# A state-space layer and a gated recurrence in one kernel: two groups' recurrences side by side in the convolution

## The chip, the cores and the metric

The kernel runs on one core of one Trainium2 chip. The metric is the device time of one execution in microseconds; the time before is the median of three runs, 2799.89 us (2799.45 to 2800.06). The core has five engines that each work through a queue of their own in order: TensorE (PE, matmuls, with PEld for its weight loads), VectorE (DVE), ScalarE (ACT), GpSimd (POOL) and SyncE (SP), which here issues nearly all DMA transfers.

## The reference

Input x is [8, 2048, 512]: 8 batch rows, 2048 positions, 512 channels. Two blocks follow each other, each with a layer norm before and after and the input added:

```
x = x + layernorm(S4(layernorm(x)))
x = x + layernorm(FFN(layernorm(x)))
```

S4 is a diagonal-plus-low-rank state-space layer with 64 states. Its convolution kernel K of length 2048 for each channel is made from the parameters, and it computes

```
h1 = irfft(rfft(r, 2L) * rfft(K, 2L))[:, :L]
return gelu(h1 + D[0] * r, approximate=False)
```

FFN reads the first axis as time (T = 8 steps here, with 2048 rows):

```
def step(c, xt):
    ft = sigmoid(xt @ wf.T + c @ uf.T + bf)
    it = sigmoid(xt @ wi.T + c @ ui.T + bi)
    gt = tanh(xt @ wc.T + c @ uc.T + bc)
    return ft * c + it * gt
c_final = scan(step, c0, x)
return tanh(x @ wo.T + c_final @ uo.T + bo)
```

c0 is one vector in_c for all rows, so its products with uf, ui and uc are three vectors of 512 that join the biases at the first step.

## The kernel before

**First stage (to about 150 us).** From the S4 parameters it computes the transition matrix A of a chunk of 128 positions and its powers, split into two float16 halves ("hi" and "lo"); all later S4 products are three float16 matmuls, hi x hi, lo x hi, hi x lo (`mm3`, L448). Beside it, `stats` (L584) loads the whole input in 32 tiles of 1 MB, through five buffers in turn, and computes means and variances: for chunk j, DVE takes nd rows of eight (`ND`, five from the sixth chunk on) and ACT the others. It also normalises groups 0 and 1 and runs their recurrences. This stage's order is chosen by a scheduler, not by hand.

**Convolution stage (to about 630 us).** The 512 channels are 16 groups of 32. The 2048 positions are 16 chunks of 128. A group needs:

- its normalised input `u`: two loads `xg` of 1 MB, then for eight pairs of chunks a subtraction on POOL (L640), a multiply on DVE (L642), a copy to float16 on ACT (L644) and the low half on POOL (L646). This is `norm_x`; it is done two groups ahead.
- the recurrence over chunks, `chain_in`, `chain_hi`, `chain_lo` (L648 to L667): for 15 chunks j, PSUM gets three products of u (L450 to L452), two with the high half of the state before (L660), and one with its low half (L666). Then `split` (L100) writes the new state x: ACT copies it to float16 (L101), DVE subtracts to get the low half (L102). Step j + 1 needs both.
- taps: `tap_steps`, twelve doublings that make 128 taps `m` for each half of the group, each with a `split`; a copy from `mb` on POOL (L682) comes first, and a 1 MB load t of the kernel's Toeplitz form (L679).
- the convolution itself: 32 calls of `conv_mm` (L698), one for a channel, six matmuls each, and eight Gelu evictions on ACT (L716), after which SP stores 2 MB of y.

In iteration g of the loop at L807, PE does the convolution of group g, in 16 slots s_ of two calls, and between them the recurrence of group g + 1, one step a slot: the high products between the two calls, the low one after the second, and the input products of the next step at the slot's end. `norm_x` for group g + 2, the taps for g + 1 and `work` stand at hand-written slots. For PE, ACT, DVE and POOL the order within an iteration is the program's order; work of neighbouring iterations may be placed across their border by the scheduler. SP's order is the scheduler's. Two pools hold the states x of two groups.

`work` is what the second block needs later. `weight_pieces` (L387) turns seven weight matrices, in 14 pieces, into Strassen-like sums with scaled float16 halves and stores them to `wf_d`: a load `wl` (512 KB), four sums on DVE in a buffer `ws` (L404, L405 in slot 2; L408, L409 in slot 5), `plain` in slot 8 (three blocks without sums, L392 on ACT and L393 on DVE, one store) and `summed` in slot 12 (four blocks, one store). The load for the next piece is issued in slot 9. `first_piece` (L442), in slot 14 of groups 1 to 12, loads 128 rows of uf, ui or uc (256 KB) and multiplies them with in_c, summing along the row (L446).

**Second block (from about 630 us).** The gate matmuls of `part_a` and `part_b` run with PE nearly without a pause; the change touches only names of buffers there.

## Time and profile before

| what | value |
|---|---|
| median of three runs | 2799.89 us |
| the profiled execution | 2797.84 us, span 2796.0 us |
| first stage, to the first convolution matmuls | about 146 to 150 us |
| convolution groups 1 to 14 | about 165 to 600 us |
| DVE, ACT, POOL busy in 300 to 400 us | 81.1, 65.9, 75.1 us |
| PE busy in 300 to 400 us | 83.3 us |
| DMA share in 300 to 400 us | 0.83, 257 GB/s |
| DMA share and rate in 0 to 140 us | 274 GB/s on average |
| L102 on DVE, one low half of x (128x256) | 0.42 us |
| L101 on ACT, one high half of x | 0.38 us |

A busy share is the part of a stretch in which the engine runs instructions. A wait is the idle time of an engine just before an instruction, put down to what released it last. In a row of the timeline the columns are start and duration in us, engine, line, operation, output and input tiles, their shapes, a count of merged instructions and, in brackets, the idle time before with its releaser. "x" is the state of the recurrence, "pxt" its PSUM tile, "m" and "pmt" taps, "pyt" the convolution's PSUM tile, "u" the normalised input, "wl", "ws", "wr", "wq" a weight piece, its sums and its converted blocks, "un" rows for the c0 products.

### The profile page before, as it was taken

Reading aid. Unit: us, or ns where it says so; the run is one execution under the profiler, and the core shown is the slowest. Engines: PE = TensorE matmul, PEld = TensorE weight load, DVE = VectorE, ACT = ScalarE, POOL = GpSimd, SP = SyncE. Lnnn points to the kernel's source line nnn. Section 1 sums busy time; section 2 is a strip of 40 time slices with the busy share of each in tenths; the row PEclk is TensorE's granted clock in tenths of the full one; section 3 lists DMA queues with packets and bytes.
Section 4 is the critical chain, followed back from the end, with each engine's and each line's share of the span. In section 5 each row is a group of like instructions: output and inputs, shape, how many; then the busy total and the mean of one; then the engine's idle time right before and its main releaser. Section 6 shows DMA issues by size and latency. Waiting matters only on the chain.

```text
span 2796.0 us, 59846 instructions
## 1 busy us (share of the span) xinstructions
PE 2538.4 (91%) x23892; PEld 2225.9 (80%) x23892; DVE 2076.8 (74%) x4208; ACT 1474.4 (53%) x3075; POOL 1224.0 (44%) x1520
## 2 busy tenths in 40 slices
PE   4578888896999999999999999999999999999990
PEld 3367777785888888888888887888888788888880
DVE  8878888867667766577887777778777577776748
ACT  8966666654444444445555544455555445544436
POOL 5767777743112211114554531355544124543317
PEclk9799999998999999999999999999999999999995
DMA  6977887887335433235665532355554335543247
GB/s 237 311 232 243 256 257 245 260 282 208 106 75 132 113 90 85 95 91 142 162 178 150 144 103 91 108 165 170 155 165 134 95 94 154 165 124 102 91 168 250
DMA packets 507535, 449.24 MB, mean 161 GB/s; under 512 B 275574, under 2 KB 386680, under 8 KB 502264
## 3 DMA queue, kind: packets, MB, share of 16 engines
q1 hardware_dynamic: 506824, 444.90, 52.9%
q8 instruction: 186, 3.05, 0.4%
q14 instruction: 93, 0.76, 0.1%
q10 hardware_dynamic: 432, 0.52, 0.1%
HBM read 293.58 MB, written 151.78 MB: 159 GB/s over the span
## 4 chain that ended last, share of the span: by engine, by line
PE 63%; DVE 6%; ACT 3%; issue 1%; POOL 1%; DMA 1%; SPq 0%; POOLq 0%; DVEq 0%; ACTq 0%
PE u L955 61%; PE pt L485 2%; DVE u L997 1%; DVE zz L1187 1%; ACT gate L1021 1%; ACT xf L101 0%; PE u L450 0%; DVE sth L462 0%; DVE u2p L994 0%; DVE xf L102 0%; PE u L452 0%; PE u L451 0%; DVE cd L1042 0%; ACT zr L1153 0%; ACT cf L1064 0%
## 5 line engine op out<-in xcount | busy, mean ns | idle before, releaser
L955 PEld LDWEIGHTS <-w 128*128 128x128 f16 x15120 | 1480.8, 98 | 203.2 <-issue 18.9
L955 PE MATMUL u<-xf,w 128*128 128x256 f16 x8064 | 944.1, 273 | 22.9 <-ACT gate L1021 9.6
L955 PE MATMUL u<-cf,w 128*128 128x256 f16 x7056 | 825.6, 273 | 1.2 <-DVE cf L1066 1.2
L1021 ACT ACTIVATE gate<-u,bias 128x512 f32<-128x512 f32 (+1 forms) x384 | 201.0, 574 | 282.4 <-PE u L955 282.1
L993 ACT ACTIVATE u2p<-u 128x256 f32<-128x256 f32 x256 | 96.6, 379 | 425.2 <-PE u L955 425.0
L955 PE MATMUL u<-w,xf 128*128 128x256 f16 x2688 | 310.8, 273 | 3.7 <-DVE u L997 3.7
L1154 POOL TENSOR_TENSOR x1r<-x1r,zr 128x512 f32<-128x512 f32 x96 | 133.5, 1391 | 407.4 <-ACT zr L1153 298.8
L994 DVE TENSOR_TENSOR u2p<-u2p,u 128x256 f32<-128x256 f32 x256 | 106.7, 417 | 275.2 <-ACT u2p L993 273.7
L909 POOL TENSOR_TENSOR xr<-y,xr 128x512 f32<-128x512 f32 x120 | 160.6, 1358 | 304.0 <-ACT y L908 304.0
L955 PEld LDWEIGHTS <-xf 128*128 128x128 f16 x2688 | 263.2, 98 | 36.1 <-DVE u L997 5.2
L997 DVE TENSOR_TENSOR u<-u,u2p 128x512 f32<-128x512 f32 x256 | 179.0, 699 | 8.8
L646 POOL TENSOR_TENSOR u<-xg,u 128x512 f16<-128x512 f32 x104 | 129.1, 1241 | 107.6 <-ACT u L644 106.6
L471 POOL TENSOR_TENSOR rsy<-rsy,nhalf 128x2 f32<-128x2 f32 (+1 forms) x68 | 50.2, 739 | 283.2 <-DVE rsy L465 282.0
L640 POOL TENSOR_TENSOR xg<-xg,mu 128x512 f32<-128x512 f32 x112 | 162.3, 1455 | 6.7 <-DMA xg<-in_xr 6.7
L102 DVE TENSOR_TENSOR x<-pxt,x 128x256 f16<-128x256 f32 x240 | 100.0, 418 | 63.6 <-ACT x L101 62.2
L1026 DVE SCALAR_TENSOR_TENSOR gate<-gate,gate 128x1024 f32<-128x1024 f32 x64 | 90.0, 1406 | 69.5 <-ACT gate L1021 68.3
L1136 POOL TENSOR_TENSOR zr<-zr,ur 128x512 f32<-128x512 f32 x96 | 131.2, 1367 | 21.1 <-DMA zr<-z_d 12.7
L462 DVE BATCH_NORM_STATS2 sty<-y 128x6 f32<-128x512 f32 x120 | 76.9, 681 | 77.1 <-DMA y<-y_d 77.1
L666 PE MATMUL pxt<-x,at 128*128 128x256 f16 x224 | 61.8, 276 | 79.4 <-DVE x L102 78.8
L101 ACT ACTIVATE x<-pxt 128x256 f16<-128x256 f32 x240 | 91.5, 382 | 74.4 <-PE pxt L666 68.7
L451 PE MATMUL pyt<-u,t 128*128 128x128 f16 (+2 forms) x544 | 124.0, 228 | 0.0
L452 PE MATMUL pyt<-u,t 128*128 128x128 f16 (+2 forms) x544 | 123.5, 227 | 0.0
(375 smaller groups left out, 5204.8 us busy)
## 6 DMA issues: line engine op xcount, KB each, us to landing
xs<-in_rr SPq DMA_DIRECT2D x32, 1024.0 KB, 6.0
t<-kpad SPq DMA_DIRECT2D x32, 1024.0 KB, 5.6
y_d<-y SPq DMA_DIRECT2D x30, 1024.0 KB, 7.6
xr<-in_r SPq DMA_DIRECT2D x60, 512.0 KB, 5.5
xa<-x_d SPq DMA_DIRECT2D x120, 256.0 KB, 4.0
y<-y_d SPq DMA_DIRECT2D x59, 512.0 KB, 5.9
x_d<-xr SPq DMA_DIRECT2D x59, 512.0 KB, 3.2
xg<-in_xr SPq DMA_DIRECT2D x28, 1024.0 KB, 8.2
```

The source lines that it names most:

```text
L102: V.tensor_tensor(lo, src, hi, ALU.subtract)
L451: T.matmul(out, lhsT=w(1), rhs=x(0), start=False, stop=False)
L452: T.matmul(out, lhsT=w(0), rhs=x(1), start=False, stop=stop)
L640: Q.tensor_tensor(xg, xg, bc(mu1), ALU.subtract)
L646: (V if g == 2 else Q).tensor_tensor(u[:, js, 1], xg, u[:, js, 0], ALU.subtract)
L909: Q.tensor_tensor(xv, yv, xv, ALU.add)
L955: T.matmul(u[:, d], lhsT=w(f, b, i == 1, k), rhs=x(f, b, i == 2, k), start=opens and bank not in seen, stop=stop and j == len(n) - 1, skip ...
L994: V.tensor_tensor(u2, u2, u[:, UY], ALU.add)
L997: V.tensor_tensor(u[:, 2:4], u[:, 2:4], u2[:, None].to_broadcast([P, 2, BP]), ALU.add)
L1021: act = lambda o, s_, b: S.activation(o, s_, AF.Tanh, scale=gsc[kind], bias=b)
L1136: Q.tensor_tensor(s_["z"], s_["z"], us_[c], ALU.add)
L1154: Q.tensor_tensor(s_["x"], s_["x"], s_["z"], ALU.add)
```

## The change

- The recurrence of group c is no longer done in one iteration. Its steps 0 to 6 are done in iteration c - 2 at positions 11, 14, 18, 21, 25, 28, 31 (a position is one `conv_mm`, two a slot), its steps 7 to 14 in iteration c - 1 at positions 3, 6, 10, 13, 16, 20, 23, 27. So two recurrences stand side by side. At each position the input, high and low products follow each other. Group 2 runs in iteration 1 alone, at every odd position; group 3 has four steps in iteration 1 and eleven in iteration 2. A third buffer for x (pool `cx`) is added.
- To make room, the four sums of a weight piece are made in place in `wl`, after the plain blocks, which stand first now; the halves of a row are swapped at loading, by two loads. The conversions are four instead of three on each of ACT and DVE, in slots 2, 3, 13 and 14, with four stores from two buffers (`wr`, `wq`) in turn; the sums stand in slots 5, 7, 9 and 11. The next piece's load is issued after slot 14.
- The c0 products leave the convolution. Their rows are loaded in the first stage, three at a time (768 KB), into the tile `ya`, which is not used yet then, at chunks 8, 9, 11 and 12, and multiplied at chunks 10 to 13, three each.
- Buffers of the second block that shared tags with `un`, `ws` and `c0r` move to a pool `FJ2`, opened when `cx` and `cr` are closed.

```diff
+    puc = const.tile([P, 3, KT], F32, name="puc")
...
         def load():
             wl = wjob[w, i] = FJ.tile([P, 2, H], F32, name="wl")
-            dma(out=wl, in_=a["wt"][w].rearrange("(a k) p m -> p k a m", a=2)[:, i])
+            wsrc = a["wt"][w].rearrange("(a k) p m -> p k a m", a=2)[:, i]
+            dma(out=wl[:, :, BP:], in_=wsrc[:, :, 0:BP])
+            dma(out=wl[:, :, 0:BP], in_=wsrc[:, :, BP:])
 
         def sums(part):
             wl = wjob[w, i]
+            a21, a11, a22, a12 = wl[:, 0, 0:BP], wl[:, 0, BP:], wl[:, 1, 0:BP], wl[:, 1, BP:]
+            o, x, y, op = ((a11, a11, a21, ALU.subtract), (a21, a21, a22, ALU.add), (a22, a22, a11, ALU.subtract), (a12, a12, a22, ALU.subtract))[part]
+            V.tensor_tensor(o, x, y, op)
+
+        def plain(part):
+            wl = wjob[w, i]
             if part == 0:
...
+                wr = FJ.tile([P, 2, 2, BP], F16, name="wr")
+                halves((wr[:, :, 0], wr[:, :, 1]), wl[:, :, BP:], sc)
+                dma(out=wf_d[WORDER.index(w), :, i, 0:2], in_=wr)
             else:
...
+                wr = FJ.tile([P, 2, BP], F16, name="wr", tag="wq")
+                halves((wr[:, 0], wr[:, 1]), wl[:, 1, 0:BP], -sc)
+                dma(out=wf_d[WORDER.index(w), :, i, 2], in_=wr)
+
+        def summed(part):
+            wl = wjob[w, i] if part == 0 else wjob.pop((w, i))
+            wq = FJ.tile([P, 2, 2, BP], F16, name="wq", tag="wq" if part else "wr")
+            halves((wq[:, :, 0], wq[:, :, 1]), wl[:, :, part * BP : (part + 1) * BP], sc)
+            dma(out=wf_d[WORDER.index(w), :, i, 3 + 2 * part : 5 + 2 * part], in_=wq)
...
+    def c0_load(n):
+
+        dma(out=yw[:, 1 + n % 2 * 3 : 4 + n % 2 * 3], in_=a["un"].rearrange("g m p h -> p (g m) h")[:, 3 * n : 3 * n + 3])
+
+    def c0_product(n):
+
+        v = yw[:, 1 + n % 6]
+        tc.keep_in_program_order(V.scalar_tensor_tensor(v, v, 1.0, yw[:, 0], ALU.mult, ALU.mult, accum_out=puc[:, n // KT, n % KT : n % KT + 1]))
...
-                xs_[g] = (ce, cb)[g % 2].tile([P, NJ - 1, 2, GB], F16, name="x", bufs=1)
+                xs_[g] = (cb, cx, ce)[g % 3].tile([P, NJ - 1, 2, GB], F16, name="x", bufs=1)
...
         for j in range(NJ):
+            if j == 8:
+                dma(out=yw[:, 0], in_=a["c0r"])
+            if j in (8, 9, 11, 12):
+                c0_load((8, 9, 11, 12).index(j))
             stats(j)
+            if 10 <= j < 14:
+                for n in range(3):
+                    c0_product(3 * (j - 10) + n)
...
-        JS = (2, 5, 8, 12)
+        JS = (2, 3, 5, 7, 9, 11, 13, 14)
...
+        HEAD, REST = (11, 14, 18, 21, 25, 28, 31), (3, 6, 10, 13, 16, 20, 23, 27)
+        steps(1, 2, 0, range(1, 2 * NJ - 1, 2))
+        steps(1, 3, 0, (18, 22, 26, 30))
+        steps(2, 3, 4, (2, 4, 7, 9, 12, 14, 17, 19, 22, 24, 27))
+        for c in range(4, NG):
+            steps(c - 2, c, 0, HEAD)
+            steps(c - 1, c, len(HEAD), REST)
+
+        def chain_at(g, p):
+            for c, j in chain.get((g, p), ()):
+                chain_in(c, j)
+                chain_step(c, j)
...
                     conv_mm(g, 2 * s_)
-                    if ahead and s_ < NJ - 1:
-                        chain_hi(g + 1, s_)
+                    chain_at(g, 2 * s_)
                     conv_mm(g, 2 * s_ + 1)
-                    if ahead and s_ < NJ - 1:
-                        chain_lo(g + 1, s_)
+                    chain_at(g, 2 * s_ + 1)
                     if ahead and 1 <= s_ <= 12:
                         tap_step(*taps[s_ - 1])
-                    if ahead and s_ < NJ - 2:
-                        chain_in(g + 1, s_ + 1)
                     for f in work.get((g, s_), ()):
                         f()
```

`yw` is the tile `ya` seen as rows of 512 channels; `at`, `work` and `conv_mm` are as before.

More of the change, by code (lines that the diff above doesn't have):

```diff
@@ L108, in s4_gated_block @@
     cb = kctx.enter_context(tc.tile_pool(name="cb", bufs=2))
-    ectx, mctx, rctx, pctx = ExitStack(), ExitStack(), ExitStack(), ExitStack()
+    ectx, mctx, rctx, xctx, pctx = ExitStack(), ExitStack(), ExitStack(), ExitStack(), ExitStack()
     ce = ectx.enter_context(tc.tile_pool(name="ce", bufs=1))
@@ L396, in load @@
             wl = wjob[w, i] = FJ.tile([P, 2, H], F32, name="wl")
-            dma(out=wl, in_=a["wt"][w].rearrange("(a k) p m -> p k a m", a=2)[:, i])
+            wsrc = a["wt"][w].rearrange("(a k) p m -> p k a m", a=2)[:, i]
+            dma(out=wl[:, :, BP:], in_=wsrc[:, :, 0:BP])
+            dma(out=wl[:, :, 0:BP], in_=wsrc[:, :, BP:])
         def sums(part):
             wl = wjob[w, i]
-            a11, a21, a12 = wl[:, 0, 0:BP], wl[:, 0, BP:], wl[:, 1, 0:BP]
+            a21, a11, a22, a12 = wl[:, 0, 0:BP], wl[:, 0, BP:], wl[:, 1, 0:BP], wl[:, 1, BP:]
@@ L402, in sums @@
+            o, x, y, op = ((a11, a11, a21, ALU.subtract), (a21, a21, a22, ALU.add), (a22, a22, a11, ALU.subtract), (a12, a12, a22, ALU.subtract))[part]
+            V.tensor_tensor(o, x, y, op)
+        def plain(part):
+            wl = wjob[w, i]
             if part == 0:
-                ws = wjob["s", w, i] = FJ.tile([P, 4, BP], F32, name="ws")
-                V.tensor_tensor(ws[:, 0], a21, wl[:, 1, BP:], ALU.add)
-                V.tensor_tensor(ws[:, 2], a11, a21, ALU.subtract)
-            else:
-                ws = wjob["s", w, i]
-                V.tensor_tensor(ws[:, 1], ws[:, 0], a11, ALU.subtract)
-                V.tensor_tensor(ws[:, 3], a12, ws[:, 1], ALU.subtract)
@@ L411, in plain @@
-        def plain():
-            wl = wjob.pop((w, i))
-            wr = FJ.tile([P, 3, 2, BP], F16, name="wr")
-            halves((wr[:, 0:2, 0], wr[:, 0:2, 1]), wl[:, :, 0:BP], sc)
-            halves((wr[:, 2, 0], wr[:, 2, 1]), wl[:, 1, BP:], -sc)
-            dma(out=wf_d[WORDER.index(w), :, i, 0:3], in_=wr)
-        def summed():
-            ws = wjob.pop(("s", w, i))
-            wq = FJ.tile([P, 4, 2, BP], F16, name="wq")
-            halves((wq[:, :, 0], wq[:, :, 1]), ws, sc)
-            dma(out=wf_d[WORDER.index(w), :, i, 3:7], in_=wq)
@@ L424, in weight_pieces @@
-        return load, lambda: sums(0), lambda: sums(1), plain, summed
+                wr = FJ.tile([P, 2, 2, BP], F16, name="wr")
+                halves((wr[:, :, 0], wr[:, :, 1]), wl[:, :, BP:], sc)
+                dma(out=wf_d[WORDER.index(w), :, i, 0:2], in_=wr)
+            else:
+                wr = FJ.tile([P, 2, BP], F16, name="wr", tag="wq")
[6 more added lines that the diff above has]
+            dma(out=wf_d[WORDER.index(w), :, i, 3 + 2 * part : 5 + 2 * part], in_=wq)
@@ L426, in out_pieces @@
+        order = ((plain, 0), (plain, 1), (sums, 0), (sums, 1), (sums, 2), (sums, 3), (summed, 0), (summed, 1))
+        return [load] + [lambda f=f, part=part: f(part) for f, part in order]
     def out_pieces(i):
@@ L440, in out_pieces @@
         return load, split_
-    def first_piece(gt, m):
-        un = FJ.tile([P, H], F32, name="un")
-        dma(out=un, in_=a["un"][gt, m])
-        V.scalar_tensor_tensor(un, un, 1.0, c0r, ALU.mult, ALU.mult, accum_out=puc[:, gt, m : m + 1])
+    def c0_load(n):
[3 more added lines that the diff above has]
+        tc.keep_in_program_order(V.scalar_tensor_tensor(v, v, 1.0, yw[:, 0], ALU.mult, ALU.mult, accum_out=puc[:, n // KT, n % KT : n % KT + 1]))
     def mm3(out, w, x, start=True, stop=True):
@@ L485, in forms @@
                 T.transpose(pt[h][:, k], xa[h][:, k * P : (k + 1) * P], ident)
-        b1 = FJ.tile([P, 2, 2, P], F32, name="b1", tag="un")
-        ts = FJ.tile([P, 4, 2, P], F32, name="ts", tag="ws")
+        b1 = FJ2.tile([P, 2, 2, P], F32, name="b1")
+        ts = FJ2.tile([P, 4, 2, P], F32, name="ts", tag="ws")
         for h in range(2):
@@ L548, in sum_ @@
             if t and cj % 2 == 0:
-                x1 = FJ.tile([P, H], F32, name="x1e", tag="ws" if cj else "wr")
+                x1 = (FJ2 if cj else FJ).tile([P, H], F32, name="x1e", tag="ws" if cj else "wr")
             early["x1", cj] = x1
@@ L557, in xnorm @@
             if cj == 1:
-                normed["o"] = FJ.tile([P, 2, H], F32, name="xa1", tag="wq")
+                normed["o"] = FJ2.tile([P, 2, H], F32, name="xa1", tag="wq")
             x = normed[cj] = normed["o"][:, cj // 2] if cj % 2 else FE.tile([P, H], F32, name="xa", bufs=2)
@@ L578, in s4_gated_block @@
     ya = cb.tile([P, QC, H // HS, 2, HS], F32, name="ya", bufs=1)
+    yw = ya.rearrange("p c (k a) t h -> p (c k) (a t h)", k=2)
     with ExitStack() as cctx:
@@ L766, in s4_gated_block @@
             split(mb[:, 0, k, :], mb[:, 1, k, :], pmt)
+        cx = xctx.enter_context(tc.tile_pool(name="cx", bufs=1, reuse_waits="tile"))
         for g in range(2):
@@ L780, in s4_gated_block @@
         jobs = [weight_pieces(w, i) for w in WORDER for i in range(2)]
-        firsts = [(gt, m) for gt in range(3) for m in range(KT)]
-        JS = (2, 5, 8, 12)
+        JS = (2, 3, 5, 7, 9, 11, 13, 14)
         work = {}
@@ L788, in s4_gated_block, with steps @@
         for n, job in enumerate(jobs):
-            if n < NG - 3:
-                at(n + 1, 0 if n == 0 else -1, job[0])
-                for s_, f in zip(JS, job[1:]):
-                    at(n + 1, s_, f)
-                if n + 1 < NG - 3:
-                    at(n + 1, 9, jobs[n + 1][0])
-            else:
-                s0 = 5 * (n - NG + 3)
-                for k, f in enumerate(job):
-                    at(NG - 2, s0 + k, f)
-        for n, (gt, m) in enumerate(firsts):
-            at(n + 1, 14, lambda gt=gt, m=m: first_piece(gt, m))
+            if n == 0:
+                at(1, 0, job[0])
+            for k, (s_, f) in enumerate(zip(JS, job[1:])):
+                at(n + 1, s_ if n < NG - 3 else k, f)
+            if n + 1 < len(jobs):
+                at(n + 1, 14, jobs[n + 1][0])
+        chain = {}
+        def steps(g, c, j0, ps_):
+            for j, p in enumerate(ps_, j0):
+                chain.setdefault((g, p), []).append((c, j))
+        HEAD, REST = (11, 14, 18, 21, 25, 28, 31), (3, 6, 10, 13, 16, 20, 23, 27)
[9 more added lines that the diff above has]
+                chain_step(c, j)
         for g in range(NG - 1):
@@ L811, in s4_gated_block @@
                 FJ = ctx.enter_context(tc.tile_pool(name="fj", bufs=1, side="right", reuse_waits="tile"))
-                c0r = FJ.tile([P, H], F32, name="c0r")
-                dma(out=c0r, in_=a["c0r"])
-                puc = FJ.tile([P, 3, KT], F32, name="puc")
             if g == NG - 2:
+                xctx.close()
                 rctx.close()
+                FJ2 = ctx.enter_context(tc.tile_pool(name="fj2", bufs=1, side="right", reuse_waits="tile"))
                 FW = ctx.enter_context(tc.tile_pool(name="fw", bufs=1, side="right", reuse_waits="tile"))
@@ L830, in s4_gated_block @@
                     taps = tap_steps(g + 1)
-                    chain_in(g + 1, 0)
                 if nn:
@@ L987, in part_a @@
         else:
-            g = gates[key] = FJ.tile([P, 4, BP], F32, name="gate2", tag="wq") if kind == 2 else FT.tile([P, 4, BP], F32, name=f"gate{kind}")
+            g = gates[key] = FJ2.tile([P, 4, BP], F32, name="gate2", tag="wq") if kind == 2 else FT.tile([P, 4, BP], F32, name=f"gate{kind}")
             c22 = g[:, 2]
@@ L1180, in load_x @@
             else:
-                s_["x"] = (FJ, FJ, FE, FT, FJ, FT)[i - 3].tile([P, 2, H], F32, name="xx", tag=("wl", "ws", "y", "gate1", "wq", "gate0")[i - 3])
+                s_["x"] = (FJ, FJ2, FE, FT, FJ2, FT)[i - 3].tile([P, 2, H], F32, name="xx", tag=("wl", "ws", "y", "gate1", "wq", "gate0")[i - 3])
             dma(out=s_["x"], in_=x1_d[c, :, 2 * tp : 2 * tp + 2])
@@ L1216, in s4_gated_block @@
         V.scalar_tensor_tensor(bias0[:, gt], puc[:, gt], 1.0 if gt == 2 else 0.5, bias[:, gt], ALU.mult, ALU.add)
-    u2p, u2s = FJ.tile([P, 2, BP], F32, name="u2p", tag="c0r"), []
+    u2p, u2s = FJ.tile([P, 2, BP], F32, name="u2p", tag="wq"), []
     todo = {}
```

## The prediction

> **What bounds the kernel now.** I read the page first (which engine is full, and where), then busy time by stage, then the waits of the matrix engine, then the timeline around the longest of them.

> ```profile
> span 2796.0 us, 59846 instructions
> PE 2538.4 (91%) x23892; PEld 2225.9 (80%) x23892; DVE 2076.8 (74%) x4208; ACT 1474.4 (53%) x3075; POOL 1224.0 (44%) x1520
> 232.60:264.45 31.85, 26.62 (x319) 22.95 (x317) 25.77 (x45) 21.02 (x46) 23.59 (x21) 1.00 0.81 253
> 296.35:328.20 31.85, 26.62 (x320) 22.95 (x318) 25.78 (x45) 21.02 (x46) 23.57 (x21) 1.00 0.81 253
> PE pxt L666 <- DVE x L102: 68.0, 65, 4.9
> PE pxt L660 <- ACT x L101: 2.9, 10, 1.5
> ```

> TensorE carries the whole run; the change touches the first 620 us only. The two rows with a colon are two convolution groups (length, then busy us of PE, PE's weight loads, DVE, ACT, POOL, then clock, DMA share and GB/s): a group takes 31.85 us, TensorE works 26.62 of it at clock 1.00, DVE 25.8, POOL 23.6. The idle 5.2 us is almost all one wait: between 160 and 600 us the last matmul of a recurrence step (L666) waited 65 times, 68.0 us in all, for the low half of the step before it (L102 on DVE). The next rows show why that half is late at a group's end (PE's last convolution matmul of this group ends near 328.2).

> ```profile
> 327.03 0.63 ACT L644 ACTIVATE u<-xg 128x512 f16<-128x512 f32 x1 [1.50 <-DVE xg L642]
> 327.74 1.16 POOL L646 TENSOR_TENSOR u<-xg,u 128x512 f16<-128x512 f32 x1 [2.43 <-ACT u L644]
> 328.85 1.24 POOL L682 COPY m<-mb 128x128 f16<-128x128 f16 x1
> 329.67 2.84 POOL L640 TENSOR_TENSOR xg<-xg,mu 128x512 f32<-128x512 f32 x2
> 324.70 1.70 DVE L393 SCALAR_TENSOR_TENSOR wq<-ws,wq 128x1024 f16<-128x1024 f32 x1 [0.26 <-ACT wq L392]
> 326.32 0.68 DVE L642 TENSOR_TENSOR xg<-xg,rs 128x512 f32<-128x512 f32 x1
> 331.31 1.75 DVE L642 TENSOR_TENSOR xg<-xg,rs 128x512 f32<-128x512 f32 x1 [0.83 <-POOL xg L640]
> 332.98 0.41 DVE L102 TENSOR_TENSOR x<-pxt,x 128x256 f16<-128x256 f32 x1
> 333.45 0.27 PE L666 MATMUL pxt<-x,at 128*128 128x256 f16 x1 [1.02 <-DVE x L102]
> ```

> DVE runs its queue in order. A normalisation multiply (L642) waits for POOL's subtraction, which waits for a copy that waits for the group's end; the recurrence's low half stands behind it and PE stands still. The same multiply takes 0.68 us while POOL waits and 1.75 while POOL works.

> **The sum's base.** The profiled execution took 2797.84 us, 1.84 more than its span; the median of the three runs is 2799.89. I work out differences from the profile and take them from the median.

> **Part 1, two recurrences side by side (groups 2 to 13, twelve of them).** Nothing is removed: 15 steps a group stay. What changes is the distance. A convolution position is six matmuls, 0.34 us (302.14 to 302.48 in PE's timeline); the three input products of a step take 0.33, its two high products 0.22, the low one 0.11. Before, steps were two positions apart; now three or four, with the other chain's steps between in mid-group. A step's latency is ACT 0.38, DVE 0.42 and about 0.3 of hand-over, 1.1 us; from position 10 to 28 the distance is 2.5 us or more, so 1.3 us of DVE lateness is absorbed. The two longest stalls there now, 1.58 and 0.97 us, come from 2.57 us (L404 and L405 together) and 1.92 us (both L393 of the plain parts) on DVE; the change also spreads these over slots. I cost the stalls of mid-group at nothing.

> At the group's end the cover is gone. In the order of the changed program, PE does the convolutions of positions 0 to 3 of the next group before the low product of the step at 31, and then the step at 3 at once; no matmul lies between the two. On DVE the low half of step 31 stands behind the first multiply (L642) of the next group. With 0 at PE's last matmul of position 31: PE reaches step 3 at 0.33 + 4 x 0.34 + 0.22 + 0.33 + 0.11 = 2.4. That multiply ended at 331.31 + 1.75 = 333.06 in the rows above, 4.86 after 328.2; the low half after it ends at 5.27. POOL's order at this place is the same (L646, copy, two L640). So PE stands 5.27 - 2.4 - 0.22 (high products) = 2.7 us. Bounds: 1.1 (the latency alone, if the multiply is in time) and 3.3 (POOL half a microsecond later, because its L646 now waits for an ACT copy behind 0.62 us of weight conversion and a 0.69 us Gelu). I take 2.7, because the rows are of this place.

> The second place is position 10. ACT's queue after step 3 (5.7 to 6.1) holds a Gelu 0.69, a copy (L644) 0.63, two small ones, and then the first weight conversion of the group, 0.62: done near 8.4. DVE takes the low part of that conversion (L393, 128x512: 1.43 us) and another multiply (0.8) before it comes to step 6: ready at 10.9. PE gets to its low product of step 10 at 5.4 + 1.8 + 2.3 = 9.5. That is 1.4; bounds 0 and 1.4, taken 1.0, since some of ACT's queue can run while PE stands at step 3. Together 3.7 us against 5.2: 1.5 us a group, **-18 us**; bounds 1.1 and 5.2, that is -49 and 0. Group 1 gets four steps more and keeps its two-position distance, group 14 gets seven fewer but starts its last weight piece in slot 0, behind a load: nothing for both (bounds -4 and +4).

> [...]

> **Part 2, weight sums in place, two store buffers.** The four sums keep their sizes (two of 256 wide at 1.07 and 1.50, two at 0.60 and 0.42 in the group at 302 us). The conversions become four (512, 256, 512, 512) for three (512, 256, 1024): one more instruction on ACT and one on DVE, 0.1 us each of fixed time, hidden in mid-group; at position 10 it is in the sum above. SP issues two loads and four stores for one and two. What can be late is the next piece's load: it needs the last conversion of the piece before (slot 14), where it used to be issued before slot 9, and ACT asks for it in slot 2. ACT behind it holds steps 6 and 10.

> ```profile
> t<-kpad SPq DMA_DIRECT2D x2, 1024.0 KB, 5.5
> wl<-in_wt SPq DMA_DIRECT2D x1, 512.0 KB, 8.1
> un<-in_un SPq DMA_DIRECT2D x1, 256.0 KB, 5.2
> ```

> These are KB and us from issue to landing. SP now has the tap load (t) and a weight store just ahead of it, and the loads go out near 2.5 to 3.0; ACT asks at 7.8. With 5.2 us of landing (256 KB each) they arrive at 8, which costs nothing to 0.5; with 8.1, near 11. I take nothing and keep +3 us a group as a rival. [...]

> **Part 3, c0 products.** They leave DVE's queue in groups 1 to 12 (12.4 us) and with them 256 KB a group; what that frees is in the walk above. They enter the first stage, between 100 and 130 us:

> ```profile
> L446 DVE SCALAR_TENSOR_TENSOR un<-un,c0r 128x512 f32<-128x512 f32 x12 | 12.4, 1032 | 0.0
> 100.00:110.00 10.00, 7.01 (x26) 3.10 (x26) 9.10 (x27) 9.46 (x29) 7.68 (x14) 0.76 0.93 335
> 110.00:120.00 10.00, 5.68 (x33) 3.18 (x33) 10.00 (x26) 9.77 (x28) 6.43 (x13) 1.00 0.98 247
> DVE st L599 <- DMA xs<-in_rr: 5.8, 5, 3.1
> DVE x L102 <- ACT x L101: 5.2, 9, 1.2
> ```

> DVE, ACT and the DMA engines are all above 0.9 there. DVE's idle time from 90 to 152 us is 5.8 us for late loads and 5.2 us for ACT after 131 us, where the products no longer run. Of 12.4 us of products, 5.8 can go into the first: +6.6. Two of the four loads of 768 KB stand in SP's queue ahead of the last tile loads, taps and xg loads, where the DMA share is 0.98 to 1.03; 1.5 MB at 250 to 330 GB/s is 5 to 6 us, mostly in the same stretch. Bounds +1.4 (all idle used) and +12.4; **+7**. From 600 us on nothing changes but buffers.

> **Sum:** 2799.89 - 18 + 7 = **2789 us**.

> **Rivals.** (a) The distance works at the group's end as well (the multiply in time, no stall at 10): -49 + 4, **2755**. For it: ACT has no 1.0 us conversion at that place, and DVE loses 1.0 us of un. Against: POOL's subtraction waits for PE's own last matmul. (b) Slower, by one mechanism: the weight load lands late. Place: ACT in slot 2; price: every microsecond past 7.8 is a microsecond at position 10, twelve times. From 1.5 us late the groups gain nothing and the first stage's 7 remain; 3 us late gives 2789 + 36 = **2825**. For it: 8.1 in the row of wl. Against: that load now goes ahead of the 1 MB xg load. (c) The gain of the groups, near 0.6 us each, is what the first stage costs: **2800**.

> **Numbers.** Forecast 0.48 (own range 2775 to 2794), (a) 0.15, (b) 0.22, (c) 0.15. Under 0.2%, 5.6 us, can't be told from no change; so faster 0.63, same 0.15, slower 0.22. The range goes from (a) to a load two microseconds late (2813): 2756 to 2812.

> **What would show it.** Groups of 30.4 us with PE busy 26.6; L666 waiting once for 2 to 3 us at each group's end and about 1 us near position 10, and not in mid-group; PE's waits from 160 to 600 us near 50 us; the first convolution 7 us later. Wrong if ACT waits for wl in each group, if the waits in mid-group stay, or if the first stage moves by more than 12 us.

## The result and the profile after

The changed kernel takes 2811.97 us (median of five runs, 2811.53 to 2813.05) against 2800.06 for the kernel before in the same session: ratio 1.0041, interval 1.0026 to 1.0056. It is slower by 11.9 us; the forecast was 2789, faster. The profiled execution took 2813.05 us. The first two lines of its page give the span and each engine's busy us and share; then come TensorE's waits from 160 to 600 us (total, times, longest). L672 is the low product now, L666 the two high ones:

```profile
span 2811.3 us, 60012 instructions
PE 2566.5 (91%) x23892; PEld 2248.8 (80%) x23892; DVE 2074.3 (74%) x4222; ACT 1474.8 (52%) x3089; POOL 1223.2 (44%) x1520
```

```profile
PE pxt L672 <- DVE x L103: 27.0, 17, 4.5
PE pxt L666 <- ACT x L102: 21.9, 15, 3.5
```

The waits fell from 71 us to 49, about what the forecast said (50). The time did not follow. The windows by stage show why (length, busy us of PE, weight loads, DVE, ACT, POOL, then TensorE's granted clock, DMA share and GB/s); two groups of the changed kernel:

```profile
305.74:336.55 30.81, 27.70 (x319) 24.15 (x317) 25.64 (x44) 20.94 (x48) 23.10 (x21) 0.94 0.88 252
336.55:367.30 30.75, 27.62 (x318) 24.00 (x316) 23.90 (x43) 20.86 (x48) 22.88 (x21) 0.94 0.88 254
```

A group lasts 30.8 us instead of 31.85. It idles 3.1 us instead of 5.2, but TensorE is busy 27.7 us instead of 26.6 with the same matmuls, and its clock is 0.94 instead of 1.00. The timeline at one group's end shows what is left of the wait: the step at 3 stands 1.19 us for ACT (behind the copy L650 and its multiply) and 1.91 us for DVE, whose low half waits behind the multiply L648, as the forecast said. Together that is 3.1 us, where it said 2.7.

```profile
307.08 0.27 PE L672 MATMUL pxt<-x,at 128*128 128x256 f16 x1
308.55 0.38 PE L666 MATMUL pxt<-x,at 128*128 128x256 f16 x2 [1.19 <-ACT x L102]
310.84 0.27 PE L672 MATMUL pxt<-x,at 128*128 128x256 f16 x1 [1.91 <-DVE x L103]
...
308.72 1.74 DVE L648 TENSOR_TENSOR xg<-xg,rs 128x512 f32<-128x512 f32 x1 [1.16 <-POOL xg L646]
310.38 0.41 DVE L103 TENSOR_TENSOR x<-pxt,x 128x256 f16<-128x256 f32 x1
...
307.60 0.63 ACT L650 ACTIVATE u<-xg 128x512 f16<-128x512 f32 x1 [1.78 <-DVE xg L648]
308.13 0.37 ACT L102 ACTIVATE x<-pxt 128x256 f16<-128x256 f32 x1
```

Now the clock around it, in stretches of 3.41 us (same columns). All changes of clock in this trace between 150 and 660 us fall on one grid of 3.413 us; these stretches lie on it:

```profile
305.10:308.52 3.42, 2.26 (x32) 2.01 (x30) 2.33 (x4) 1.64 (x5) 3.42 (x3) 1.00 0.73 202
308.52:311.93 3.41, 1.47 (x22) 1.26 (x22) 2.44 (x4) 1.34 (x4) 3.18 (x4) 1.00 0.89 229
311.93:315.34 3.41, 3.41 (x31) 3.03 (x29) 1.51 (x4) 2.25 (x7) 2.39 (x2) 0.50 1.12 362
315.34:318.76 3.42, 3.42 (x49) 3.26 (x48) 3.42 (x8) 2.85 (x8) 1.66 (x2) 1.00 1.09 240
```

In the stretch with the wait TensorE is busy 0.43; in the next it runs at half speed, 31 matmuls where the one after has 49. A group is nine such stretches long (30.8 / 3.413 = 9.02), so it meets the same one each time. In the kernel before the waits were more but scattered: no stretch of a steady group was under 0.52, and the clock stayed at 1.00. The emptiest there from 175 to 600 us, and the one after it (same columns, kernel before):

```profile
197.04:200.45 3.41, 1.77 (x26) 1.61 (x25) 2.64 (x4) 1.84 (x4) 3.37 (x3) 1.00 0.39 155
200.45:203.87 3.41, 2.77 (x40) 2.46 (x38) 2.70 (x5) 1.40 (x3) 3.41 (x4) 1.00 0.63 187
```

The end of the convolution is 11.2 us late. The issues of the y_d stores (y_d is the convolution's output in memory, two stores a group, so they mark each group's time) show where: the first is 9.5 us later (166.50 against 156.96); from it to the second store of group 2, groups 0 to 2 take 81.6 us against 79.0 (+2.7); groups 3 to 11 take 276.9 against 286.5 (-9.6); from there to the last y_d store 115.4 against 106.8 (+8.6).

First stage, two windows and the rows of the new loads and products:

```profile
100.00:110.00 10.00, 7.65 (x29) 3.75 (x29) 9.04 (x32) 8.91 (x29) 7.41 (x12) 0.64 0.95 345
110.00:120.00 10.00, 5.15 (x21) 2.60 (x21) 10.00 (x28) 8.96 (x25) 7.06 (x10) 0.70 0.91 255
...
L451 DVE SCALAR_TENSOR_TENSOR ya<-ya 128x512 f32<-128x512 f32 x12 | 7.6, 675 | 0.0
...
ya<-in_un SPq DMA_DIRECT2D x4, 768.0 KB, 7.9
```

The products cost 0.68 us each there, not the 1.03 of the groups. And the waits of the last part, 583 to 640 us, ACT's and TensorE's:

```profile
ACT wq L393 <- DMA wf_d<-wr: 7.7, 1, 7.7
...
ACT wr L393 <- DMA wl<-in_wt: 4.4, 1, 4.4
```

```profile
PE pmt L455 <- DVE m L103: 6.1, 1, 6.1
PE pxt L666 <- ACT x L102: 4.8, 2, 3.5
```

In group 14 the last weight piece runs in slots 0 to 7. Its load and its first store are issued around two weight loads of 1.8 MB; the third conversion needs the buffer of that store, which was issued at 592.5, and ACT stands until 607.0. Behind ACT wait DVE and then TensorE.

### The profile page after: what moved, and what is told of

Its sections match the earlier page's. It is cut to its first block, busy times and chain, and to the rows that moved or that the text cites. A ratio compares the mean times of both kernels' runs of the same rounds, so it can differ in the third digit from the quotient of the medians.

```text
span 2811.3 us, 60012 instructions
## 1 busy us (share of the span) xinstructions
PE 2566.5 (91%) x23892; PEld 2248.8 (80%) x23892; DVE 2074.3 (74%) x4222; ACT 1474.8 (52%) x3089; POOL 1223.2 (44%) x1520
## 4 chain that ended last, share of the span: by engine, by line
PE 62%; DVE 6%; ACT 3%; issue 1%; POOL 1%; DMA 1%; SPq 0%; POOLq 0%; DVEq 0%; ACTq 0%
PE u L976 60%; PE pt L490 2%; DVE zz L1208 1%; ACT gate L1042 1%; DVE u L1018 1%; ACT xf L102 0%; DVE sth L467 0%; POOL xr L930 0%; PE u L455 0%; DVE cd L1063 0%; DVE xf L103 0%; DVE u2p L1015 0%; DVE gate L1062 0%; PE u L457 0%; PE u L456 0%
## 5 line engine op out<-in xcount | busy, mean ns | idle before, releaser
L1015 DVE TENSOR_TENSOR u2p<-u2p,u 128x256 f32<-128x256 f32 x256 | 106.7, 417 | 270.8 <-ACT u2p L1014 269.5
L930 POOL TENSOR_TENSOR xr<-y,xr 128x512 f32<-128x512 f32 x120 | 160.7, 1360 | 297.8 <-ACT y L929 296.9
L646 POOL TENSOR_TENSOR xg<-xg,mu 128x512 f32<-128x512 f32 x112 | 159.5, 1430 | 18.2 <-DMA xg<-in_xr 18.1
L648 DVE TENSOR_TENSOR xg<-xg,rs 128x512 f32<-128x512 f32 x112 | 127.9, 1143 | 16.2 <-POOL xg L646 16.2
L102 ACT ACTIVATE x<-pxt 128x256 f16<-128x256 f32 x240 | 91.2, 381 | 86.2 <-PE pxt L672 82.5
L455 PE MATMUL pyt<-u,t 128*128 128x128 f16 (+2 forms) x544 | 127.5, 234 | 3.8 <-ACT u L627 3.8
L457 PE MATMUL pyt<-u,t 128*128 128x128 f16 (+2 forms) x544 | 127.9, 235 | 0.5 <-POOL u L628 0.5
L456 PE MATMUL pyt<-u,t 128*128 128x128 f16 (+2 forms) x544 | 128.2, 236 | 0.0
## 6 DMA issues: line engine op xcount, KB each, us to landing
xs<-in_rr SPq DMA_DIRECT2D x32, 1024.0 KB, 6.9
t<-kpad SPq DMA_DIRECT2D x32, 1024.0 KB, 6.3
y_d<-y SPq DMA_DIRECT2D x30, 1024.0 KB, 8.5
xr<-in_r SPq DMA_DIRECT2D x60, 512.0 KB, 6.1
xa<-x_d SPq DMA_DIRECT2D x120, 256.0 KB, 4.2
y<-y_d SPq DMA_DIRECT2D x59, 512.0 KB, 6.4
x_d<-xr SPq DMA_DIRECT2D x59, 512.0 KB, 3.2
xg<-in_xr SPq DMA_DIRECT2D x28, 1024.0 KB, 9.2
```

The lines of the kernel that those rows point to most:

```text
L455: T.matmul(out, lhsT=w(0), rhs=x(0), start=start, stop=False)
L456: T.matmul(out, lhsT=w(1), rhs=x(0), start=False, stop=False)
L457: T.matmul(out, lhsT=w(0), rhs=x(1), start=False, stop=stop)
L646: Q.tensor_tensor(xg, xg, bc(mu1), ALU.subtract)
L648: V.tensor_tensor(xg, xg, bc(rs1), ALU.mult)
L930: Q.tensor_tensor(xv, yv, xv, ALU.add)
```

## The experiments

Times are medians; the kernel before took 2799.99 to 2800.94 beside them in the same sessions. "Group" is the mean length of groups 3 to 11, and "tail" runs from group 11's second y_d store to the last of the convolution, both from one profiled execution.

| kernel | time, us | first y_d store | group | tail |
|---|---|---|---|---|
| before | 2800.06 | 157.0 | 31.83 | 106.8 |
| changed | 2811.97 | 166.5 | 30.77 | 115.4 |
| own | 2805.46 | 167.8 | 30.68 | 108.4 |
| c0_none | 2803.30 | 158.1 | 30.89 | 115.7 |
| c0_loads | 2810.67 | 165.3 | 30.72 | 116.2 |
| shift | 2804.00 | 166.4 | 30.10 | 114.9 |
| norm_after | 2805.85 | 169.0 | 30.32 | 113.0 |
| fill | 2811.24 | 167.1 | 30.73 | 115.7 |
| chain_old | 2807.17 | 167.4 | 30.81 | 115.4 |
| na_d2_own | 2801.14 | 167.3 | 30.98 | 105.2 |
| js | 2826.04 | 169.1 | 31.68 | 116.7 |
| fill_js | 2824.38 | 167.6 | 31.57 | 117.6 |
| chain_old_js | 2805.78 | 168.1 | 30.50 | 114.4 |
| best1 | 2808.07 | 160.4 | 31.61 | 109.4 |
| bf_noc0 | 2798.70 | 160.7 | 31.58 | 106.7 |
| bf_p2 | 2798.57 | 158.9 | 30.37 | 117.6 |
| nosums | 2814.30 | 167.2 | 30.80 | 114.8 |
| best_old | 2793.08 | 158.1 | 30.43 | 114.4 |
| bf_p2_last | 2785.62 | 158.8 | 30.52 | 103.8 |
| best_shift | 2785.59 | 159.8 | 30.59 | 102.0 |

The first store of one and the same first stage differs by 1 to 4 us between executions (before, bf_noc0, bf_p2); shift and best_shift, whose groups 3 to 11 run the same code, differ by 0.5 us a group in the one execution that was profiled, so differences up to that are not read either.

**own.** In `summed`, for the last piece only:

```diff
-wq = FJ.tile([P, 2, 2, BP], F16, name="wq", tag="wq" if part else "wr")
+wq = FJ2.tile([P, 4, 2, BP], F16, name="wq", tag="wq" if part else "ws")[:, 0:2]
```

> The changed kernel, except that the two conversions of the sums of the very last weight piece (group 14) write to buffers of their own instead of the two that still wait for their stores. Theory A (the store wait in group 14 is the failed step): the scalar engine's 7.7 us wait for wf_d<-wr goes, and with it the 6.1 us wait of TensorE for m and one or two half-clock windows; 5 to 9 us less than the changed kernel, 2803 to 2807 us. Rival (the two 1.8 MB weight loads beside it are what costs, and the wait was only their shadow): within 2 us of 2812.

6.5 us less, the tail 7.0 shorter, and TensorE's 6.1 us wait for m is gone. The store wait costs about what it seemed to; the 4.4 us wait for the load is still there.

**c0_none and c0_loads.** The loads and products of the first stage taken out, or the products alone:

```diff
-            if j in (8, 9, 11, 12):
-                c0_load((8, 9, 11, 12).index(j))
...
-            if 10 <= j < 14:
-                for n in range(3):
-                    c0_product(3 * (j - 10) + n)
```

> The changed kernel without the four loads of un, the load of c0r and the twelve c0 products (their result is set to zero, so this part of the computation is left out). Theory A (the products and loads in the first stage cost what the first convolution is late): the first y_d store comes at about 157 us instead of 166.5, and the time is 8 to 10 us below the changed kernel, 2802 to 2804 us. Rival (the shift is of the order of work in that stage, or is absorbed by the convolution groups later): first store at 160 us or later, or a time within 4 us of 2812.

> The changed kernel with the loads of un and c0r in the first stage but without the twelve c0 products (their result is set to zero, so this part of the computation is left out). Theory C (the vector engine's 12.4 us of products cost what the first convolution is late, the loads nothing): first y_d store at 157 to 159 us, time within 2 us of 2803. Rival (the loads' 3.25 MB ahead of the last tile loads, at a DMA share of 0.9 to 1.03, cost 5 us or more): first y_d store at 162 to 166 us, 2808 us or more.

Without both the first store comes 8.4 us earlier and the time is 8.7 lower. Without the products alone it is 1.2 us earlier and 1.3 lower. So the 3.25 MB of loads cost some 7 of the 8.5 us, the products about one: theory C was wrong.

**shift and norm_after.** Other positions for the steps, or the block with `norm_x` moved behind the two `conv_mm` and `chain_at` of a slot:

```diff
-        HEAD, REST = (11, 14, 18, 21, 25, 28, 31), (3, 6, 10, 13, 16, 20, 23, 27)
+        HEAD, REST = (9, 12, 16, 19, 23, 26, 29), (4, 7, 11, 14, 17, 20, 24, 27)
```

> The changed kernel with the recurrence steps put at other positions: first seven at 9, 12, 16, 19, 23, 26, 29 instead of 11, 14, 18, 21, 25, 28, 31, last eight at 4, 7, 11, 14, 17, 20, 24, 27 instead of 3, 6, 10, 13, 16, 20, 23, 27, so that seven positions and not four lie across a group's end. Theory B (the half-speed window in each group follows from a 3.41 us window in which TensorE is busy under about half, which the one long stall at the group's end makes): the stall falls from 3.1 to about 1.8 us, no window of a steady group stays under 0.45, the clock stays at 1.00, and a group takes 27.8 to 28.3 us instead of 30.8; 2770 to 2778 us. Rival (the half-speed windows come from TensorE being denser): a denser TensorE has as many or more of them, a group gains 1.3 us at most, 2795 us or more.

> The changed kernel with the normalisation of the group after next issued behind the two convolution positions and steps of a slot instead of ahead of them, so that the first multiply of a group stands behind the low half of the step at position 3, and the last ones behind the step at 31. Theory B: the waits of 1.2 and 1.9 us at the group's end fall to 1 us together, the half-speed window goes, groups of 27.5 to 29 us, 2760 to 2790 us. Rival 1 (the clock drops for density, not for idleness): half-speed windows stay, 2790 us or more. Rival 2 (the low half is only held up by the next instruction in line, a weight conversion or the last multiply): the same 3 us of waits at another position, 2805 us or more.

Both are faster by 6 to 8 us, and both far from what I expected. In shift the wait at a group's end is 2.4 us, once, and most of the groups still have a half-speed window. In norm_after the wait is split (0.2, 0.5, 0.3 to 1.8 and 0.4 to 1.4 us) and sums to 2.2 to 2.9 us a group: its rival 2 held, nearly the same wait at other positions. There the three groups without a half-speed window, 369 to 457 us, took 28.9, 29.4 and 29.5 us by their second y_d stores, those on either side, with one, 31.0.

**fill.** Surplus work where TensorE stands:

```diff
+            if g >= 4 and j == 7:
+                for _ in range(3):
+                    mm3(pxs[g, j], lambda i: bm16[:, i, :], lambda i: u[:, j, i, :])
             mm3(pxs[g, j], lambda i: bm16[:, i, :], lambda i: u[:, j, i, :], stop=(j == 0))
```

> The changed kernel with more work for TensorE: the three input products of the step at position 3 are issued three times more than needed (nine matmuls, about 1.0 us, in each of twelve groups; the last three overwrite what the others wrote), at the place where TensorE stands still for 1.2 and 1.9 us. Theory B (a 3.41 us window in which TensorE is busy under about 0.46 is followed by one at half speed): the window at the group's end goes from 0.13 to 0.44 busy to 0.42 to 0.73, most half-speed windows of the groups go, and although there is more to do each group without one is 1.2 to 1.7 us shorter; 2790 to 2800 us. Rival 1 (the clock drops because TensorE is denser): no window goes, 2811 us or more. Rival 2 (the half-speed window costs nothing, since another engine sets the group's length): the windows go and the time stays within 3 us of 2812.

From 282 to 592 us there is no half-speed window at all, although TensorE has 1.0 us more to do in each group; the emptiest stretch from 282 to 470 us was busy 0.48, where the changed kernel has 0.43 and less. Here the half-speed windows went with the idleness, not with density. But the time is the same, as rival 2 had it: the half-speed window alone does not set a group's length. One group's window, then the wait at position 10 and rows of DVE and ACT ahead of it (timeline; L675 is the low product in this run, L669 the high ones):

```profile
417.00:447.80 30.80, 27.23 (x325) 23.76 (x324) 25.49 (x43) 20.79 (x48) 21.92 (x20) 1.00 0.88 250
```

```profile
439.39 0.27 PE L675 MATMUL pxt<-x,at 128*128 128x256 f16 x1 [1.44 <-DVE x L103]
...
436.81 1.59 DVE L394 SCALAR_TENSOR_TENSOR wr<-wl,wr 128x512 f16<-128x512 f32 x1 [1.06 <-ACT wr L393]
438.32 0.68 DVE L648 TENSOR_TENSOR xg<-xg,rs 128x512 f32<-128x512 f32 x1
438.92 0.41 DVE L103 TENSOR_TENSOR x<-pxt,x 128x256 f16<-128x256 f32 x1
...
436.14 0.63 ACT L393 ACTIVATE wr<-wl 128x512 f16<-128x512 f32 x1 [0.65 <-ACT m L102]
```

A wait of 1.44 us came up at position 10, behind the weight conversion and the multiply, as the prediction's "second place" had it. ACT stood 0.65 us before that conversion. The profile names m; in five of nine groups it names the weight load. In the changed kernel TensorE's half-speed stretch lies just before position 10 and TensorE comes there later. So one stall seems to cover the other; no run takes both away and nothing else.

**chain_old.** `chain_at` replaced by the old calls (`chain_hi` after the first position of a slot, `chain_lo` after the second, `chain_in` of the next step at the slot's end).

> The changed kernel with the recurrences in the old order again (one at a time, a step every two positions, high products and low product in different positions), the weight pieces and the c0 products as changed. Theory A (the recurrences' new order gave about 1.05 us a group, the loss is in the first stage and in group 14): groups of 31.5 to 32 us and no half-speed window in them; 10 to 16 us above the changed kernel, and more if the old order in group 14 stands behind the scalar engine's 7.7 us wait; 2822 to 2835 us. Rival (the new order gives nothing, the in-place sums and the removed c0 products do): 2808 to 2816 us.

The rival held, if a little below its range: with the old order the groups take 30.81 us, with the new 30.77. The time is even 4.8 us lower with the old order, since groups 0 to 2 take 75.8 us with it and 81.6 with the new. Nine groups of each in one window, the old order first, then the changed kernel:

```profile
274.55:550.50 275.95, 239.84 (x2827) 206.36 (x2827) 214.33 (x387) 185.94 (x421) 208.04 (x180) 1.00 0.86 253
```

```profile
274.96:552.10 277.14, 248.77 (x2832) 216.41 (x2830) 222.24 (x388) 188.18 (x424) 207.40 (x181) 0.94 0.87 253
```

Idle per group: 36.1 / 9 = 4.0 us in the old order, 28.4 / 9 = 3.2 in the new; busy 26.6 and 27.6. In this sum, what the new order saves in waits the clock takes. It is much the same in groups 0 to 2, between the stores named above, the old order first:

```profile
167.38:243.20 75.82, 63.83 (x759) 55.55 (x758) 56.70 (x97) 47.91 (x105) 52.89 (x46) 0.95 0.84 242
```

```profile
166.50:248.14 81.64, 69.23 (x782) 59.76 (x781) 61.78 (x102) 49.64 (x110) 55.01 (x47) 0.91 0.80 232
```

TensorE idles 12.0 us in the old order and 12.4 in the new, and is busy 63.8 and 69.2 us, with 23 matmuls more and the clock at 0.91 instead of 0.95. The old order has a cost of its own with these weight pieces: in each of the nine groups ACT stands 1.9 to 3.0 us before the conversion that reads the load wl (the profile names the load in five of them), and TensorE's high products behind it wait 1.1 to 2.2 us for ACT.

```profile
ACT wr L393 <- DMA wl<-in_wt: 11.3, 5, 2.7
ACT wr L393 <- issue: 9.8, 4, 3.0
```

**na_d2_own.** Own buffers, the normalisation behind the steps of a slot and from slot 2 on, and the head of the recurrence at 13, 16, 19, 22, 25, 28, 31.

> Three edits on the changed kernel: own buffers for the last piece's sums; the normalisation of the group after next issued behind the steps of a slot and only from slot 2 on; the first seven steps of a recurrence at 13, 16, 19, 22, 25, 28, 31 so that their inputs are ready. Theory B: nothing of the normalisation stands ahead of the steps at 31 and 3, the stall at the group's end falls to 1 us or less, no half-speed windows in the groups, groups of 27.5 to 28.5 us; 2765 to 2785 us. Rival (GpSimd, 23.2 us of 30.8 busy and idle at the group's start now, then falls behind later in the group, and the step at 6 or 10 waits for it instead): groups of 30 us or more, 2795 us or more.

Few half-speed windows, but groups of 31.0 us, as the rival's number had it. From 275 to 555 us L672 stood for DVE in 33 waits of up to 1.0 us (20.1 us in all), and ACT stood 1.5 to 3.9 us in each group for the load wl, which the rival did not name. The gain in time, 10.8 us, is a shorter tail (by 10.2 us, of which own alone has 7.0) and shorter groups 0 to 2 (77.4 us against 81.6).

**js, fill_js, chain_old_js.** The first conversions later, on the changed kernel, on fill and on chain_old:

```diff
-        JS = (2, 3, 5, 7, 9, 11, 13, 14)
+        JS = (4, 5, 7, 8, 9, 11, 13, 14)
```

> The changed kernel with the first conversions of each weight piece later: slots 4, 5, 7, 8, 9, 11, 13, 14 instead of 2, 3, 5, 7, 9, 11, 13, 14, so that the scalar engine asks for the loaded piece two slots (about 3.5 us) later. Theory D (a group has two bounds that cover each other: TensorE's own time with the half-speed window, 27.7 busy and 3.1 idle, and the loop from the last conversion over the load of the next piece to the step at position 10): taking away the loop alone leaves the other, groups of 30.6 to 30.9 us, within 4 us of 2811. Rival (the late load alone sets the group): groups of 29.5 us or less, 2795 us or less.

> Both at once: three times three surplus input products at position 3, which keep the half-speed window away, and the first conversions at slots 4 and 5. Theory D: with both bounds gone the 1.4 us wait at position 10 that came with the surplus products goes too; groups of 29.2 to 29.7 us, 2790 to 2798 us. Rival (the normalisation, with GpSimd 23 us of 30.8 busy and its waits for the scalar engine, sets the group whatever TensorE does): groups of 30.4 us or more, 2806 us or more.

> The old order of the recurrences on the changed kernel, and the first conversions at slots 4 and 5. With theory D the new order is worth something only where neither the half-speed window nor the late load covers it: here groups stay at 30.0 to 30.7 us because a step every two positions waits in mid-group, against 29.2 to 29.7 in the run with surplus products; 2800 to 2807 us. Rival (the new order is worth nothing at all): groups of 29.7 us or less.

ACT no longer waited for wl, yet with the new order the groups grew by 0.8 to 0.9 us, which theory D had in neither run (in fill_js the number is its rival's, in js nobody's); a wait came up at a later step (1.17 us in js, 1.72 in fill_js), among the conversions' new slots. With the old order they took 30.50 us against 30.81, too little to read. The later conversions were no clean way to take the load's wait away, so what would hold a group without half-speed windows stays open.

**bf_noc0, bf_p2, nosums.** The kernel before without un and the products of the groups; the kernel before with the changed weight pieces alone; the changed kernel without the four sums (`V.tensor_tensor(o, x, y, op)` left out but for the last piece, about 2.1 us a group).

> The kernel before without the loads of un and the c0 products of groups 1 to 12 (their sums are set to zero, so this part is left out). Theory E (the vector engine's queue sets a group's length in either order of the recurrences, so a microsecond of its work taken out shortens the group by about a microsecond): 12.4 us of products gone, groups of 30.8 us instead of 31.85, 2786 to 2791 us. With it the 1.05 us a group that the change gained would all be the products' removal. Rival (the products in slot 14 stand beside waits and cost nothing; the gain is the spread of the weight pieces): 2797 us or more.

> The kernel before with the changed weight pieces alone (sums in place, six smaller steps a slot or two apart, stores from two buffers in turn, the load of the next piece in slot 14); recurrences and c0 products as before. Theory E: the same amount of work on the vector engine, so groups of 31.6 to 32.2 us; the store wait of group 14 comes with it, 5 to 9 us; 2803 to 2812 us. Rival (the spread of the pieces gives the 1.05 us a group): groups of 31.2 us or less, 2798 us or less.

> The changed kernel without the four sums of the weight pieces in groups 1 to 13 (2.15 us a group on the vector engine; the sums are left out, loads, conversions and stores stay). Theory E: the group shortens by 1 to 2.2 us although TensorE has exactly the same work, 2783 to 2798 us. Rival (TensorE with its half-speed window sets the group, 27.7 us busy and the 3.1 us at the group's end): groups within 0.4 us of 30.8, 2806 us or more.

Theory E fell in all three. The products' removal is worth 0.25 us a group, too little to read; 2.1 us less of sums on DVE is worth nothing; and the weight pieces alone shorten a group by 1.46 us, at least as much as the whole change does (1.06). Of the two longest mid-group waits, the one of 0.97 us is gone in bf_p2; near the place of the 1.58 us TensorE still waits 1.1 to 2.5 us in seven of eight groups (296 to 545 us), now behind the piece's first conversion, which itself stood 0.8 to 2.4 us for the load wl; 1.9 us stay at a group's end. Nine groups of bf_p2:

```profile
267.84:541.87 274.03, 240.80 (x2838) 207.79 (x2836) 227.35 (x406) 185.99 (x424) 212.05 (x181) 0.99 0.89 264
```

TensorE idles 33.2 / 9 = 3.7 us a group there, with clock 0.99. But the tail is 10.8 us longer than before: ACT waits 5.9 us for wl and 4.4 us for the store of wr in group 14.

```profile
ACT wr L392 <- DMA wl<-in_wt: 5.9, 1, 5.9
ACT wq L392 <- DMA wf_d<-wr: 4.4, 1, 4.4
```

So the change can be put together from runs, each against the kernel before beside it: the weight pieces alone -2.4 us (bf_p2), with the c0 products moved as well +7.1 (chain_old), with the new order as well +11.9. The pieces give 2.4 us, the moved products and their buffers cost 9.5, the new order costs 4.8.

**best1, best_old, best_shift, bf_p2_last.** The first three have own buffers, and load un in group 0, half into ya and half into the x tile of group 2, with the products in slots 5 to 14 (the first copy of y into ya, `early_y`, moves from slot 10 to 15 of group 0); beside that best1 is fill_js, best_old is chain_old_js, best_shift is shift. bf_p2_last is bf_p2 with own buffers. It and best_shift start the last piece later:

```diff
-                at(n + 1, s_ if n < NG - 3 else k, f)
+                at(n + 1, s_ if n < NG - 3 else (4, 4, 5, 5, 6, 6, 7, 8)[k], f)
```

> The run with both, and with own buffers for the last piece's sums, and with the loads of un and c0r and the twelve products moved from the first stage into group 0 (slots 5 to 14), where the DMA share is 0.31. Theory: 6 us less for group 14 and 7 to 9 us less for the first stage than the run with both: 2776 to 2785 us, below both kernels. Rival (in group 0 the loads delay the 2 MB of xg for group 2 and so the start of group 1): first y_d store at 157 to 159 us but group 1 ends no earlier than in the changed kernel, 2785 to 2792 us.

> The old order of the recurrences, the changed weight pieces with the first conversions at slots 4 and 5, own buffers for the last piece's sums, and the loads of un and c0r and the products in group 0 instead of the first stage. From its parts: 2805.8 for the old order with the later conversions, less 6 to 8 for the last piece, less 7.7 for the first stage: 2788 to 2793 us, below both kernels. Rival (the parts don't add, since in the old order group 14 waits for its recurrence anyway): 2796 us or more.

> The kernel before with the changed weight pieces, and with the last piece mended: its first conversions start in slot 4 of group 14 instead of slot 0 (the scalar engine waited 5.9 us there for its load) and its sums go to buffers of their own (it waited 4.4 us there for a store). Theory F (the weight pieces alone give the 1.4 us a group, and what they lose, 13.4 us from the last group of the twelve to the end of the convolution, is these two waits): 8 to 12 us less than without the mending, 2786 to 2791 us, faster than both kernels. Rival (the loss there is the order of DMAs behind the two 1.8 MB weight loads, whatever the scalar engine waits for): 2795 us or more.

> The changed kernel with two recurrences side by side at the other positions (9, 12, 16, 19, 23, 26, 29 and 4, 7, 11, 14, 17, 20, 24, 27), the last piece mended as in the other run, and the loads of un and c0r and the products in group 0. If the order side by side is worth something once its steps stand better, the groups stay at 30.1 us and the two mendings take 7.7 and 8 us from 2804: 2786 to 2790 us. If it isn't, 2793 us or more, no better than the old order with the same mendings (2793).

Moving un to group 0 takes 7.2 us off the first store (fill_js to best1) and costs nothing later. best1 missed because fill_js, which it stands on, had; the two mendings took 16.3 us off that. bf_p2_last, best_shift and best_old beat both kernels: ratios 0.9946 (0.9933 to 0.9960), 0.9948 (0.9936 to 0.9961) and 0.9972 (0.9961 to 0.9984). best_old's gain over chain_old_js is in the first stage; its tail stays at 114.4 us, with ACT still waiting 6.0 us for wl, so the own buffers alone gave nothing there. In bf_p2_last one of ACT's two waits in group 14 is left, and short:

```profile
ACT wr L392 <- DMA wl<-in_wt: 1.4, 1, 1.4
```

The tail fell by 13.8 us and the time by 13.0, a little more than theory F had. best_shift met its forecast of 2786 to 2790 us, but not by groups of 30.1 us: it had half-speed windows in most groups and no shorter groups than best_old (30.6 and 30.4). It is 7.5 us faster than best_old because of the tail (102.0 against 114.4), where the last piece's slots differ too. The one sign of a gain from the order itself is shift, 30.10 us a group against 30.81 in chain_old with the same weight pieces; with the same positions best_shift has 30.59, so a gain in the groups is not shown.

## Why the prediction was wrong

- **Part 1, two recurrences, -18 us: the step that failed.** The wait at the group's end was right in place and size (2.7 predicted, 3.1 measured), the one at position 10 too (1.0; 1.44 in fill). Two things are missing. The base: the 5.2 us of waits of the kernel before fall to 4.0 without any new order (chain_old), so 0.9 us were left to gain. And the clock: I kept TensorE's busy time at 26.6 us, that is the clock at 1.00, for the changed groups. The waits that the change left stand in one place, that stretch falls to 0.43 busy, and the next runs at half speed, 1.0 us more busy time a group. Measured for the order: 0.0 us a group, and 4.8 us more in all, nearly all of it in groups 0 to 2. The clock is not the whole cause: in fill it stays at 1.00 and the group is no shorter, since a wait at position 10 takes its place. What holds the group then is open.
- **Part 2, weight pieces, "nothing" in steady groups.** Missed: -1.46 us a group alone, the whole gain of the change in the groups, and +10.8 us in the tail. I had seen that long DVE instructions of the old pieces made the two longest mid-group waits (1.58 and 0.97 us) and credited the order for absorbing them; in bf_p2, with the pieces spread and the old order, the second is gone and the first stands behind the late load instead of the sums. That DVE's late halves come from where long instructions stand and not from their sum fits nosums and js: 2.1 us less work changed nothing, the same conversions two slots later cost 0.9 us.
- **Rival (b), the load of wl late.** The load is late in steady groups too, by 0.5 us a group and more of ACT's time (4.9 us in nine groups are put down to it), but with no wait of TensorE over 0.25 us behind it in the changed kernel. The two loads of 256 KB landed 6.3 us after their issue in the median, where the prediction took 5.2 from the row of un. In chain_old, TensorE does stand behind it, 1.1 to 2.2 us a group, and in the changed kernel ACT stands 4.4 us for it in group 14.
- **Groups 1 and 14, "nothing", bounds -4 and +4.** Groups 0 to 2 cost 2.7 us, and 5.8 against the old order on the same rest. The tail costs 8.6, of which own takes back 7.0. I named that the piece starts in slot 0 behind a load, and didn't follow its store: buffer wr is used again two conversions later, and its store is issued behind 3.6 MB of weight loads and landed 14.5 us after its issue. That those loads held it up is read from the order of issue; no run moved them.
- **Part 3, first stage, +7 (bounds 1.4 and 12.4).** Measured 8.7 by c0_none: right in size, wrong in reason. I put 6.6 of it on DVE's products and let the loads hide; the products cost 1.3 and the loads the rest, where the DMA share was already above 0.9.
- **The multiply beside POOL.** 0.68 us alone and 1.74 beside POOL's work in the changed kernel, where the prediction's rows have 0.68 and 1.75. Why it is longer there no run shows; the forecast used the measured time.
- **Range.** 2812 was its upper end and the result lies just inside it by luck: that end stood for a load two microseconds late in every group, and the loss came from the first stage, the tail and the order instead.

## What to carry to other kernels

Waits of TensorE should be judged by where they fall as well as by their sum: 3.1 us in one place cost a half-speed stretch in each group, 4.0 to 5.2 us scattered (chain_old, the kernel before) did not. When a buffer is used again, follow the store that frees it through its queue at the places where the schedule is not the steady one, the last iteration above all. And try each part of a change alone: here a part meant only to make room gave all of the gain in the groups and lost most of it again at the last piece, while the new order and the moved products cost 4.8 and 9.5 us.

## What the runs showed of the hardware

The one exception is in the last convolution, at 619 us in the changed kernel, after a stretch that counts as fully busy with 79 matmuls. The shapes there (busy us, mean ns), the two kinds of columns:

```profile
L455 PE MATMUL pyt<-u,t 128*128 128x32 f16 x13 | 2.8, 215 | 0.0
...
L456 PE MATMUL pyt<-x,m 128*128 128x24 f16 x12 | 2.1, 173 | 0.0
```

They have 24 and 32 columns and follow each other every 3.41 / 79 = 43 ns, where those with 120 and 128 columns take 57 (six in 0.34 us). What lowered the clock after them no run shows.
